# Half of the down weights transposed in the final FFN, with fewer filler transposes and three weight casts on ScalarE

## The chip, the cores and the metric

The kernel runs on one core of a Trainium2 chip. A core has five engines, each with its own queue of instructions that it runs in order: TensorE (PE; its weight loads are listed apart as PEld), VectorE (DVE), ScalarE (ACT), GpSimd (POOL) and SyncE (SP, which only issues transfers here). Engines wait for each other through semaphores. SBUF is the working memory, PSUM the memory that TensorE writes its results to, and DMA moves data between them and the main memory.

The metric is the time of one execution on the device, in microseconds (us); less is better.

## The reference

A graph attention layer and a quantised feed-forward network (FFN), one after the other, each on a layernorm of its input and added to it. 384 nodes, 1024 features, 16 heads of 64, an FFN of width 352.

```python
q = x @ wq.T + bq;  k = x @ wk.T + bk;  v = x @ wv.T + bv
q2 = heads(q @ wiq.T + biq);  k2 = heads(k @ wik.T + bik);  v2 = heads(v @ wiv.T + biv)
mask = full((N, N), -inf); mask[src, dst] = softplus(edge_type_weights)[edge_type - 1]   # diagonal filled
attn = softmax(q2 @ k2^T / 8 + mask)
out = merge(attn @ v2) @ wo.T + bo
...
xq = act_fake_quant(x, clip_x)              # one scale for the whole tensor, from max |x|
gate = xq @ weight_fake_quant(w_gate).T     # one scale per row of a weight, from its max |w|
up   = xq @ weight_fake_quant(w_up).T
h = act_fake_quant(silu(gate) * up, clip_down)
y = h @ weight_fake_quant(w_down).T
...
x = x + gnn(layernorm(x));  x = x + ffn(layernorm(x))
```

`weight_fake_quant` divides a row by its scale, rounds to integers of 8 bits and multiplies by the scale again. The kernel keeps the integers as bf16 for the matmuls and applies the scales to the products.

## The kernel before

**Phase 1 (to about 170 us)** projects q, k, v and the inner q with one level of a Strassen-like scheme. `project2` (L179) handles two blocks of 128 output features at a time with seven products; each product is four accumulating matmuls of 128x192 (L190). In order they use the left operands `wa` left half, `s2`, `wa` right half, `s1`, `wb` left half, `wa` right half (changed in place by the subtraction of L211 after the third product), `wb` right half. DVE makes the sums and differences: those of the weights in `left_sums` (L170, L172, L174), those of the activations in `right_sums` (L158), and the adds of the products (L201, L207, L218, L219, L222). ScalarE makes the first copy (L204) and the one with a bias (L214). Beside that DVE computes for each edge whether a later edge has the same key (L424 to L434), and POOL scatters the edges' values into the mask in main memory (L437) and loads it back (L451).

**The attention phase (to about 325 us)** goes over eight pairs of heads. For a pair it issues on PE, in an order written out by hand, the scores (L625), the transposes of the pair before (L655, copied to SBUF by ScalarE at L657), their products with the values (L663), and as filling work either an inner-k projection (`project2` again, now with two PSUM buffers for the products), an inner-v block (L602) or parts of the output projection (L673). DVE adds the mask and takes the minimum of the negated scores (L631), ScalarE takes the exponential (L635), DVE rescales (L645).

**The FFN's weights** are prepared in between by the generator `ffn_weights` (L523), in fourteen units, here called u0 to u13: three row blocks of the gate weights, three of the up weights, eight of the down weights. A unit's row comes by a DMA on SP's queue (L533) into one of three row buffers, two units ahead. `quantise_rows` (L510) then takes the row maximum on DVE (`wmx`, L512), makes the scale (L513) and its reciprocal (`wrs`, L515) there, quantises to int8 on ScalarE (`w8b`, L518, one buffer) and casts to bf16 on DVE (`wqi`, L520, two buffers). One step later PE transposes the result (L550 for gate and up, eight transposes a unit; L557 for down, three a unit), and ScalarE copies the transposes to `wgT`, `wuT` (L551) or `wdT` (L558, L559). Which step runs when is set by `prepare` (L722) inside the pairs.

The order on PE, SP and POOL is that of the program throughout. The order on DVE and ScalarE is the program's in the first phase's opening and from L758 on; for the FFN's preparation and the attention phase a scheduler places their instructions by its own estimates, each engine still in one fixed order.

**The end (from about 325 us)**: the output projection's last products (L838) with residual and row statistics on DVE (L767 to L820), then the final FFN. There PE transposes the normalised rows (L872), spreads the greatest row maximum over the partitions with one transpose (`all_max`, L129, and a maximum on DVE, L131), and DVE and ScalarE quantise the activations (L902 to L908). Gate and up matmuls (L920) run in four groups; `silu` on ScalarE (L926), the product and its maximum on DVE (L927, L930). The same `all_max` gives the scale of h, h is quantised (L955 to L960), the down matmuls run (L969), DVE scales the products (L973), and `x` is added: the first three blocks on POOL (L977), the last three on DVE (L981), each stored by a DMA on SP's queue (L978, L982). Between these steps `keep_busy` (L874) issues transposes of an identity whose results nobody reads: 14 at L882, 14 at L890, 17 at L939. The PSUM pool `ps_x` hands out four buffers in turn to the transposes of the second row block, the fillers, the up products and every other down product.

Of the kernel before, what the change touches and what calls it, by code (L numbers as in the profile page):

```python
# [24 lines left out]
BF16 = mybir.dt.bfloat16  # L25
# [3 lines left out]
ALU = mybir.AluOpType  # L29
# [3 lines left out]
P = 128  # L33
N = 384
NT = N // P
F = 1024
KC = F // P
# [5 lines left out]
HN = N // 2  # L43
HK = KC // 2
WARM = 36
H = 16
D = F // H
I = 352
ICS = [(0, 128), (128, 128), (256, 96)]
# [12 lines left out]
def gnn_ffn_kernel(ctx: ExitStack, tc: tile.TileContext, a: dict, out: bass.AP):  # L62
    nc = tc.nc
# [6 lines left out]
    rows_p = ctx.enter_context(tc.tile_pool(name="rows", bufs=3))  # L70
# [12 lines left out]
    x = act.tile([P, NT, F], F32, name="actT")  # L83
# [10 lines left out]
    ident = const.tile([P, P], F32)  # L94
# [39 lines left out]
    w_scale = ffn.tile([P, 2, 3], F32)  # L134
    wd_scale = ffn.tile([P, KC], F32)
# [6 lines left out]
    ident_b = const.tile([P, P], BF16)  # L142
# [104 lines left out]
    with ph1_stack:  # L247
# [46 lines left out]
        def turn(t, xn, g):  # L294
            pt = ps_tp.tile([P, 4, P], F32, name="tp")
            for j in range(4):
                c = 4 * g + j
                nc.tensor.transpose(pt[:, j, :], xn[:, c * P : (c + 1) * P], ident)

            for j in range(0, 4, 2):  # L300
                c = 4 * g + j
                nc.scalar.copy(xnT[:, c : c + 2, t * P : (t + 1) * P], pt[:, j : j + 2, :])
# [10 lines left out]
        pt = ps_tp.tile([P, P], F32, name="tp")  # L313
        for _ in range(WARM):
            nc.tensor.transpose(pt, ident, ident)  # L315
# [37 lines left out]
        pt = ps_tp.tile([P, 512], F32, name="tp")  # L353
# [10 lines left out]
        pt = ps_tp.tile([P, 3, EC], F32, name="tp")  # L364
# [138 lines left out]
    ffn_w = ctx.enter_context(tc.tile_pool(name="ffn_w", bufs=1))  # L503
    wgT = ffn_w.tile([P, KC, I], BF16)
    wuT = ffn_w.tile([P, KC, I], BF16)
    wdT = ffn_w.tile([P, 3, F], BF16)
    v2 = act.tile([P, NT, F], F32, name="actT")
    outT = act.tile([P, KC, N], F32, name="actT")

    def quantise_rows(wn, rows, n, scale):  # L510
        mx = small.tile([P, 1], F32, name="wmx")
        nc.vector.tensor_reduce(mx[:rows], wn[:rows, :n], axis=AX.X, op=ALU.max, apply_absolute_value=True)  # L512
        nc.vector.tensor_scalar(scale, mx[:rows], 1.0 / QMAX, None, op0=ALU.mult)  # L513
        rs = small.tile([P, 1], F32, name="wrs")
        nc.vector.reciprocal(rs[:rows], scale)  # L515

        w8b = rows_p.tile([P, F], I8, name="w8b", bufs=1)
        nc.scalar.activation(w8b[:rows, :n], wn[:rows, :n], AF.Copy, scale=rs[:rows])  # L518
        wq = rows_p.tile([P, F], BF16, name="wqi", bufs=2)
        nc.vector.tensor_copy(wq[:rows, :n], w8b[:rows, :n])  # L520
        return wq

    def ffn_weights():  # L523

        units = [(name, m, ic) for m, name in enumerate(("L0_ffn_w_gate", "L0_ffn_w_up")) for ic in range(3)]
        units += [("L0_ffn_w_down", 2, c) for c in range(KC)]
        ahead = []

        def load_row():
            name, m, j = units[len(ahead)]  # L530
            i0, rows = ICS[j] if m < 2 else (j * P, P)
            wn = rows_p.tile([P, F], F32, name="row")
            nc.sync.dma_start(wn[:rows, : F if m < 2 else I], a[name][i0 : i0 + rows, :])  # L533
            ahead.append(wn)

        load_row()
        load_row()
        yield
        for u, (name, m, j) in enumerate(units):
            wn = ahead[u]  # L540
            if len(ahead) < len(units):
                load_row()
            if m < 2:
                i0, rows = ICS[j]
                wT = (wgT, wuT)[m]
                wq = quantise_rows(wn, rows, F, w_scale[:rows, m, j : j + 1])
                yield
                pt = ps_tp.tile([P, KC, P], BF16, name="tp")
                for k in range(KC):
                    nc.tensor.transpose(pt[:, k, :rows], wq[:rows, k * P : (k + 1) * P], ident_b[:rows, :rows])  # L550
                nc.scalar.copy(wT[:, :, i0 : i0 + rows], pt[:, :, :rows])  # L551
            else:
                wq = quantise_rows(wn, P, I, wd_scale[:, j : j + 1])
                yield
                pt = ps_tp.tile([P, 3, P], BF16, name="tp")
                for ic, (i0, rows) in enumerate(ICS):
                    nc.tensor.transpose(pt[:rows, ic, :], wq[:, i0 : i0 + rows], ident_b)  # L557
                nc.scalar.copy(wdT[:, 0:2, j * P : (j + 1) * P], pt[:, 0:2, :])  # L558
                nc.scalar.copy(wdT[:96, 2, j * P : (j + 1) * P], pt[:96, 2, :])  # L559

    prep = ffn_weights()

    next(prep)
    nc.sync.dma_start(biv_b, row_bcast(a["L0_gnn_biv"], F))

    with ExitStack() as ph:
# [19 lines left out]
        def inner_v(c):  # L586

            cs = slice(c * 256, (c + 1) * 256)
            wt = []
            for j in range(2):  # L590
                wt.append(w.tile([P, F], F32, name="wt"))
                nc.sync.dma_start(
                    wt[j].rearrange("p (k o) -> p k o", k=HK),
                    a["wiv"][j * HK : (j + 1) * HK, :, cs].rearrange("k p o -> p k o"),
                )

            def steps():
                for t in range(NT):
                    pm = ps_mm.tile([P, 256], F32, name="mm")
                    for k in range(KC):  # L600
                        k0 = k % HK * 256
                        nc.tensor.matmul(  # L602
                            pm, vT[:, k, t * P : (t + 1) * P], wt[k // HK][:, k0 : k0 + 256],
                            start=(k == 0), stop=(k == KC - 1),
                        )
                        if k < KC - 1:
                            yield
                    nc.vector.tensor_add(v2[:, t, cs], pm, biv_b[:, cs])
                    yield

            return steps()
# [58 lines left out]
        def out_group(wo, t, g, ks, pm):  # L670
            gs = slice(g * 512, (g + 1) * 512)
            for k in ks:
                nc.tensor.matmul(  # L673
                    pm, outT[:, k, t * P : (t + 1) * P], wo[k][:, gs], start=(k == 0), stop=(k == KC - 1)
                )
                yield
# [5 lines left out]

        NP = H // 2

# [3 lines left out]
        for p in range(NP):  # L688
# [4 lines left out]
            if p == NP - 1:  # L693
                early = [(t, g, ps_mm.tile([P, 512], F32, name="mm")) for t, g in ((0, 0), (0, 1))]
                fill, n = (s for t, g, pm in early for s in out_group(wo, t, g, range(NP - 2), pm)), 2 * (NP - 2)
            elif p % 2:
                k2_next, fill = inner_k(p + 1)
                n = 7 * HK + 1
            else:
                fill, n = inner_v(p // 2), NT * KC  # L700
            if p == NP - 2:

                x = act.tile([P, NT, F], F32, name="actT")
# [4 lines left out]
                for t in range(NT):  # L708
                    for g in range(2):
                        gs = slice(g * 512, (g + 1) * 512)  # L710
# [112 lines left out]
        for t in range(NT):  # L823
# [7 lines left out]
            for g, (c0, width) in enumerate(groups):  # L831
                pm = open_groups.get((t, g)) if t < NT - 1 else None
                ks = [NP - 1]
                if pm is None:
                    pool, name = (ps_mm, "mm") if g < 2 else (ps_sc, "sc")
# [14 lines left out]
    with ExitStack() as ph:  # L850
        ff = ph.enter_context(tc.tile_pool(name="ff", bufs=3))
        ps_x = ph.enter_context(tc.tile_pool(name="ps_x", bufs=4, space=PSUM))
# [9 lines left out]
        pt = ps_x.tile([P, 512], F32, name="x")  # L862
# [11 lines left out]
        def keep_busy(n, pool, name):  # L874

            pt = pool.tile([P, P], F32, name=name)
            for _ in range(n):
                nc.tensor.transpose(pt, ident, ident)

        turn(0)  # L880
        turn(1)
        keep_busy(14, ps_x, "x")  # L882
        nc.vector.tensor_scalar(
            xn[:, NT - 1, :512], x[:, NT - 1, :512], mean, rstd, op0=ALU.subtract, op1=ALU.mult
        )
# [1 line left out]
        rx = small.tile([P, 1], F32, name="ar0")  # L887
        nc.vector.reciprocal(rx, sx)
        turn(2)
        keep_busy(14, ps_x, "x")  # L890
        gu_scale = small.tile([P, 2, 3], F32, name="gu_scale")
        nc.gpsimd.tensor_scalar(gu_scale, w_scale, sx, None, op0=ALU.mult)

# [3 lines left out]
        def part(tile, t, g):  # L897
            return tile[:, 4 * g : 4 * g + 4, t * P : (t + 1) * P]

        for g in range(2):  # L900
# [6 lines left out]
            for t in ((2, 0, 1), (0, 1, 2))[g]:  # L907
                nc.vector.tensor_copy(part(xqT, t, g), part(x8, t, g))  # L908


        idle = small.tile([P, 1], F32, name="idle")
        nc.scalar.activation(idle, clip[:, 0:1], AF.Silu)
        for col, ic, c0, width in ((0, 0, 0, N), (1, 1, 0, N), (2, 2, 0, N // 2), (3, 2, N // 2, N // 2)):
            i0, rows = ICS[ic]
# [18 lines left out]
        for g in range(2):  # L933
            pt = ps_tp.tile([P, 4, P], F32, name="tp")
# [1 line left out]
                c = 4 * g + j  # L936
                nc.tensor.transpose(pt[:, j, :], wd_scale[:, c : c + 1].to_broadcast([P, P]), ident)
            nc.scalar.copy(wd_scale_b[:, g * 512 : (g + 1) * 512], pt.rearrange("p a b -> p (a b)"))
        keep_busy(17, ps_x, "x")  # L939
        mx = small.tile([P, 1], F32, name="hmax")  # L940
        scaled = small.tile([P, 4], F32, name="hscaled")
        nc.vector.tensor_tensor_reduce(
# [2 lines left out]
        pt = ps_tp.tile([P, P], F32, name="tp")  # L945
# [15 lines left out]
        last = []  # L961
        for t in range(NT):
            ts = slice(t * P, (t + 1) * P)
            for g in range(2):
                gs = slice(g * 512, (g + 1) * 512)
                pool, name = (ps_mm, "mm") if g == 0 else (ps_x, "x")
# [5 lines left out]
                y = ff.tile([P, 512], F32, name="y", bufs=6)  # L972
# [4 lines left out]
                    nc.gpsimd.tensor_add(y, x[:, t, gs], y)  # L977
                    nc.sync.dma_start(out[t * P : (t + 1) * P, gs], y)  # L978

        for t, gs, y in last:  # L980
            nc.vector.tensor_add(y, x[:, t, gs], y)  # L981
            nc.sync.dma_start(out[t * P : (t + 1) * P, gs], y)  # L982


# [45 lines left out]
```

## Time and profile before

| what | value |
|---|---|
| median of 3 runs | 374.53 us (374.22 to 374.98) |
| the profiled execution, its own time | 375.57 us |
| its span, first to last instruction | 372.7 us |
| mean granted TensorE clock in it | 0.995 |
| busy: PE, DVE, ACT, POOL | 359.5, 257.1, 115.5, 76.0 us |
| the end of the residual stage and the final FFN, first transpose of L872 to end of span | 342.0 to 372.7 us |
| row loads of w_down on the chain that ended last | 3% of the span |

Sums are made against the profiled execution, whose time is 2.87 us above its span. A row of the timeline gives the start in us, the duration in us, the engine, the line, the operation, the tiles (output, then inputs), shapes and count; in square brackets stand the idle time of the engine before it and the instruction that ended it. Records of matmuls in f32 come in pairs, two for an instruction. The matmuls' ends are modelled, so the distance from start to start is the better measure of what one holds of PE.

### The profile page before, as it was taken

Reading aid. Unit: us, or ns where it says so; the run is one execution under the profiler, and the core shown is the slowest. Engines: PE = TensorE matmul, PEld = TensorE weight load, DVE = VectorE, ACT = ScalarE, POOL = GpSimd, SP = SyncE. Lnnn points to the kernel's source line nnn. Section 1 sums busy time; section 2 is a strip of 40 time slices with the busy share of each in tenths; the row PEclk is TensorE's granted clock in tenths of the full one; section 3 lists DMA queues with packets and bytes.
Section 4 is the critical chain, followed back from the end, with each engine's and each line's share of the span. In section 5 each row is a group of like instructions: output and inputs, shape, how many; then the busy total and the mean of one; then the engine's idle time right before and its main releaser. Section 6 shows DMA issues by size and latency. Waiting matters only on the chain.

```text
span 372.7 us, 5875 instructions
## 1 busy us (share of the span) xinstructions
PE 359.5 (96%) x2112; PEld 299.9 (80%) x2113; DVE 257.1 (69%) x785; ACT 115.5 (31%) x275; POOL 76.0 (20%) x81
## 2 busy tenths in 40 slices
PE   8999999999999999989999999999999999999981
PEld 8999999999999998888887868686866545449660
DVE  5788878888889969986497357717492621099665
ACT  2352110000000003023482556445444533033630
POOL 6010355455444543430000000000000000000003
PEclk9999999999999999999999999999999999999998
DMA  7969333443333377551170040050294000000004
GB/s 234 393 249 371 130 115 113 116 134 115 113 113 115 113 267 224 176 152 68 38 233 15 19 133 20 21 170 0 96 381 130 36 0 2 0 0 4 0 0 169
DMA packets 17804, 44.50 MB, mean 119 GB/s; under 512 B 3262, under 2 KB 8400, under 8 KB 17392
## 3 DMA queue, kind: packets, MB, share of 16 engines
q1 hardware_dynamic: 15104, 39.46, 31.4%
q0 software_dynamic: 2672, 4.68, 3.9%
q8 instruction: 16, 0.26, 0.3%
q14 instruction: 12, 0.10, 0.1%
HBM read 41.91 MB, written 2.21 MB: 118 GB/s over the span
## 4 chain that ended last, share of the span: by engine, by line
PE 76%; DVE 16%; DMA 3%; ACT 2%; issue 1%; DVEq 0%; POOL 0%; POOLq 0%; ACTq 0%
PE p L190 33%; PE mm L190 8%; PE mm L602 8%; PE tp L655 4%; PE sc L625 3%; PE sc L663 3%; PE mm L673 3%; PE sc L673 3%; PE mm L307 3%; DMA row<-in_L_ffn_w_down_dram 3%; PE tp L315 2%; DVE wmx L512 1%; DVE e L645 1%; DVE st L774 1%; PE mm L920 1%
## 5 line engine op out<-in xcount | busy, mean ns | idle before, releaser
L437 POOL DMA_INDIRECT mask_d<-value,place x51 | 60.5, 1186 | 65.2 <-DVE place L434 45.9
L190 PE MATMUL p<-actT,wt 128*128 128x192 f32 x360 | 66.2, 327 | 1.0 <-DVE wt L211 1.0
L190 PEld LDWEIGHTS p<-actT,wt 128*128 128x128 f32 x360 | 59.5, 190 | 1.8 <-DVE wt L211 1.5
L602 PE MATMUL mm<-wt,actT 128*128 128x256 f32 x192 | 46.1, 384 | 0.0
L602 PEld LDWEIGHTS mm<-wt,actT 128*128 128x128 f32 x192 | 34.8, 190 | 7.8 <-issue 2.2
L635 ACT ACTIVATE e<-s,mn 128x384 f32<-128x384 f32 x48 | 29.0, 605 | 28.2 <-DVE mn L631 28.1
L631 DVE CUSTOM_DVE_ANT_0 s<-sc,mask 128x384 f32<-128x384 f32 x48 | 24.4, 552 | 15.0 <-PE sc L625 14.9
L190 PE MATMUL p<-x_right,s 128*128 128x192 f32 x176 | 32.2, 326 | 0.0
L190 PE MATMUL p<-x_right,wt 128*128 128x192 f32 x176 | 32.2, 326 | 0.0
L855 POOL MEMSET hT<- 128x384 f32 x1 | 0.4, 418 | 154.7 <-PE sc L663 154.7
L190 PEld LDWEIGHTS p<-x_right,s 128*128 128x128 f32 x176 | 29.2, 190 | 0.0
L190 PEld LDWEIGHTS p<-x_right,wt 128*128 128x128 f32 x176 | 29.2, 190 | 0.0
L657 ACT COPY eTs<-tp 128x384 f32<-128x384 f32 x48 | 20.5, 478 | 25.3 <-PE tp L655 25.3
L424 DVE SCALAR_TENSOR_TENSOR junk<-key_b,key,later 128x384 f32<-128x384 f32 (+3 forms) x51 | 27.5, 539 | 0.0
L204 ACT COPY actT<-p 128x192 f32<-128x192 f32 x15 | 4.8, 321 | 64.7 <-PE p L190 64.7
L201 DVE SCALAR_TENSOR_TENSOR actT<-p,bias,actT 128x192 f32<-128x192 f32 x45 | 18.6, 414 | 7.7 <-PE p L190 4.5
L214 ACT ACTIVATE actT<-p,bias 128x192 f32<-128x192 f32 x15 | 6.3, 420 | 50.8 <-PE p L190 29.3
L655 PEld LDWEIGHTS tp<-ident,e 128*128 128x128 f32 x144 | 17.1, 141 | 4.9 <-issue 2.4
L655 PE MATMUL tp<-ident,e 128*128 128x128 f32 x144 | 19.7, 273 | 0.3 <-ACT eTs L657 0.3
L625 PE MATMUL sc<-k,actT 64*128 64x384 f32 x96 | 20.0, 519 | 0.0
L190 PE MATMUL mm<-actT,wt 128*128 128x192 f32 x96 | 19.0, 330 | 0.0
L645 DVE TENSOR_SCALAR e<-e,rs 128x384 f32<-128x384 f32 x48 | 17.2, 415 | 0.4
(220 smaller groups left out, 593.2 us busy)
## 6 DMA issues: line engine op xcount, KB each, us to landing
wt<-in_wq_dram SPq DMA_DIRECT2D x8, 512.0 KB
wt<-in_wk_dram SPq DMA_DIRECT2D x8, 512.0 KB
wt<-in_wv_dram SPq DMA_DIRECT2D x8, 512.0 KB
wt<-in_wiq_dram SPq DMA_DIRECT2D x8, 512.0 KB
wt<-in_wik_dram SPq DMA_DIRECT2D x8, 512.0 KB
wt<-in_wiv_dram SPq DMA_DIRECT2D x8, 512.0 KB
wt<-in_wo_dram SPq DMA_DIRECT2D x8, 512.0 KB
actT<-in_x_dram SPq DMA_DIRECT2D x6, 512.0 KB
```

The costliest lines, as they stand in the source:

```text
L190: nc.tensor.matmul(z, left[:, k * P : (k + 1) * P], r[:, k, :], start=(k == 0), stop=(k == HK - 1))
L201: nc.vector.scalar_tensor_tensor(dst, z, b, with_, op0=ALU.add, op1=ALU.add)
L424: nc.vector.scalar_tensor_tensor(junk[:, :left], keys[:, (c - k0) * P : (c - k0) * P + left], key[:, c : c + 1], later[:, :left], op0=ALU. ...
L437: ins = nc.gpsimd.indirect_dma_start(out=mask_d, out_offset=bass.IndirectOffsetOnAxis(ap=place[:, c : c + 1], axis=0), in_=value[:, c : c ...
L602: nc.tensor.matmul(pm, vT[:, k, t * P : (t + 1) * P], wt[k // HK][:, k0 : k0 + 256], start=(k == 0), stop=(k == KC - 1),)
L625: nc.tensor.matmul(ps[t, h], q2[hs, t * P : (t + 1) * P], k2[hs, :], start=True, stop=True)
L631: nc.vector.tensor_tensor_reduce(s, ps[t, h], mask[:, t, :], -SCALE, 3.0e38, op0=ALU.add, op1=ALU.min, accum_out=mn[h][:, t : t + 1],)
L635: nc.scalar.activation(e[h][:, t, :], s, AF.Exp, bias=mn[h][:, t : t + 1], scale=-1.0, accum_out=sm[h][:, t : t + 1],)
L645: nc.vector.tensor_scalar(e[h][:, t, :], e[h][:, t, :], rs[:, t : t + 1], None, op0=ALU.mult)
L655: nc.tensor.transpose(pt[:, t * P : (t + 1) * P], e[h][:, t, m * P : (m + 1) * P], ident)
L657: nc.scalar.copy(eT[h][m], pt)
L673: nc.tensor.matmul(pm, outT[:, k, t * P : (t + 1) * P], wo[k][:, gs], start=(k == 0), stop=(k == KC - 1))
```

## The change

Three edits to the FFN's weights and activations, and one to the last add.

- The last four down units (u10 to u13) are cast into a tile of their own, `wd_late`, and not transposed in the attention phase. Their twelve transposes stand in the final FFN: six after the second block of rows has been turned, six after the third. DVE copies them to `wdT` behind the casts of the activations, in four copies.
- The fillers there become 10 and 9, written into a PSUM tile that exists already, where there were 14 and 14; before the transpose that spreads the maximum of h there are 7 where there were 17.
- The casts to bf16 of the three gate units (u0 to u2) are issued on ScalarE in place of DVE.
- The first of the last three adds is issued as `scalar_tensor_tensor` with a factor of 1.0.

```diff
+LATE = 4
...
+    wd_late = ffn_w.tile([P, LATE, I], BF16)
...
-    def quantise_rows(wn, rows, n, scale):
+    def quantise_rows(wn, rows, n, scale, on_scalar=False, wq=None):
...
-        wq = rows_p.tile([P, F], BF16, name="wqi", bufs=2)
-        nc.vector.tensor_copy(wq[:rows, :n], w8b[:rows, :n])
+        if wq is None:
+            wq = rows_p.tile([P, F], BF16, name="wqi", bufs=2)
+        if on_scalar:
+            nc.scalar.copy(wq[:rows, :n], w8b[:rows, :n])
+        else:
+            nc.vector.tensor_copy(wq[:rows, :n], w8b[:rows, :n])
...
-                wq = quantise_rows(wn, rows, F, w_scale[:rows, m, j : j + 1])
+                wq = quantise_rows(wn, rows, F, w_scale[:rows, m, j : j + 1], on_scalar=u < 3)
...
+            elif j >= KC - LATE:
+                quantise_rows(wn, P, I, wd_scale[:, j : j + 1], wq=wd_late[:, j - KC + LATE, :])
+                yield
...
+        def turn_late(j):
+            pl = ps_x.tile([P, 2, 3, P], BF16, name="x")
+            for u in range(2):
+                for ic, (i0, rows) in enumerate(ICS):
+                    nc.tensor.transpose(pl[:rows, u, ic, :], wd_late[:, j + u, i0 : i0 + rows], ident_b)
+            return pl
+
+        def copy_late(j, pl):
+            c0 = (KC - LATE + j) * P
+            for i0, i1, rows in ((0, 2, P), (2, 3, 96)):
+                nc.vector.tensor_copy(
+                    wdT[:rows, i0:i1, c0 : c0 + 2 * P].rearrange("p i (u q) -> p i u q", u=2),
+                    pl[:rows, :, i0:i1, :].rearrange("p u i q -> p i u q"),
+                )
+
+        def keep_turning(n, to):
+            for _ in range(n):
+                nc.tensor.transpose(to, ident, ident)
+
         turn(0)
         turn(1)
-        keep_busy(14, ps_x, "x")
+        late_a = turn_late(0)
+        keep_turning(10, pt[:, :P])
...
         turn(2)
-        keep_busy(14, ps_x, "x")
+        keep_turning(9, pt[:, :P])
+        late_b = turn_late(2)
...
+        copy_late(0, late_a)
+        copy_late(2, late_b)
...
-        keep_busy(17, ps_x, "x")
+        keep_busy(7, ps_x, "x")
...
-        for t, gs, y in last:
-            nc.vector.tensor_add(y, x[:, t, gs], y)
+        for n, (t, gs, y) in enumerate(last):
+            if n == 0:
+                nc.vector.scalar_tensor_tensor(y, x[:, t, gs], 1.0, y, op0=ALU.mult, op1=ALU.add)
+            else:
+                nc.vector.tensor_add(y, x[:, t, gs], y)
```

The compiled order of the instructions moves with it where the scheduler decides. On DVE the maximum of u2 stands where u1's cast was and that of u3 where u2's was; the reciprocals of u2 and u3, and the maxima of u4 and u5, come correspondingly earlier, and u3's cast stands ahead of u6's maximum. On ScalarE u2's quantising stands ahead of a copy with a bias that it followed, u2's cast between two copies of `wgT`, and the quantising of u10, u11 and u12 directly behind each other. SP's and POOL's orders are the same as before.

## The prediction

> **What bounds the kernel now.** I read the page first (its head and the chain that ended last), then the timeline of each stage that the change touches, TensorE (PE) ahead of the others.
>
> ```profile
> span 372.7 us, 5875 instructions
> ...
> PE 76%; DVE 16%; DMA 3%; ACT 2%; issue 1%; DVEq 0%; POOL 0%; POOLq 0%; ACTq 0%
> ```
>
> PE carries the chain except where VectorE (DVE) does; so a step is worth something where it lies on PE with no wait behind it, or on DVE where PE waits. PE's timeline at the end of phase 1 (start, us, engine, line; the idle time before a group and what ended it in brackets):
>
> ```profile
> 146.48 1.46 PE L190 MATMUL p<-right,wt 128*128 128x192 f32 x8
> 148.36 1.57 PE L190 MATMUL p<-actT,wt 128*128 128x192 f32 x8 [0.42 <-DVE wt L211]
> ...
> 152.96 1.57 PE L190 MATMUL p<-right,s 128*128 128x192 f32 x8 [0.43 <-DVE s L172]
> ...
> 158.96 1.57 PE L190 MATMUL p<-actT,wt 128*128 128x192 f32 x8 [0.53 <-DVE wt L211]
> ...
> 167.56 1.57 PE L190 MATMUL mm<-k_right,wt 128*128 128x192 f32 x8 [0.53 <-DVE k L201]
> ```
>
> A product (4 matmuls, 8 records) takes 1.30 us start to start where nothing waits. Here four begin 0.58, 0.59, 0.69 and 0.70 late, and the steps after them are longer by 0.66 together (0.11 three times, 0.23 and 0.10 after the last): 3.2 us, all for DVE, whose queue shows why:
>
> ```profile
> 146.70 0.69 DVE L520 CAST wqi<-w8b 128x1024 bf16<-128x1024 int8 x1
> ...
> 147.63 0.68 DVE L211 TENSOR_TENSOR wt<-wt,s 128x512 f32<-128x512 f32 x1
> ...
> 148.64 0.68 DVE L520 CAST wqi<-w8b 128x1024 bf16<-128x1024 int8 x1
> ...
> 153.37 1.20 DVE L512 TENSOR_REDUCE wmx<-row 128x1 f32<-128x1024 f32 x1
> ...
> 165.96 1.22 DVE L512 TENSOR_REDUCE wmx<-row 96x1 f32<-96x1024 f32 x1 [0.82 <-DMA row<-in_L_ffn_w_up_dram]
> ```
>
> DVE has no pause from 140.3 to 164.2, and the FFN's casts and maxima stand ahead of what PE waits for. The final FFN, all engines:
>
> ```profile
> 357.31 1.89 PEld L878 LDWEIGHTS x<-ident 128*128 128x128 f32 x17
> ...
> 358.03 0.08 DVE L942 DVE_READ_ACCUMULATOR2_ANT hmax<- 128x1 f32 x1
> 359.16 0.14 PEld L129 LDWEIGHTS tp<-ident,hmax 128*128 128x128 f32 x1
> ```
>
> The maximum of h is ready at 358.11, but the transpose that spreads it (L129) queues behind 17 filler transposes until 359.16.
>
> **The change, part by part.** FFN units are u0 to u13 (three gate, three up, eight down).
>
> *Three casts to ScalarE (ACT).* The compiled order of each engine's instructions lets the queue be replayed with the start-to-start times of the rows. Off DVE: u0's and u1's casts, 0.60 each (148.64 to 149.24). But the maxima of u2 and u3 (1.13 each) move up into their places. First stall: L201 takes 146.70, L211 147.03 to 147.71, PE's product starts at its natural 147.78: 0.58 gained. Second: until L172 DVE lost 1.20 and got u3's 1.13, so s2 is ready at the same 152.9 and PE starts at 152.95: what was gained is lost again. Third: now those 1.13 are missing behind, L211 ends at 157.83, natural start 158.26 instead of 158.96; 0.81 with the shorter next step. Fourth: L201 at 167.10 stood behind u5's maximum, which waited for its row; that load was issued at 161.90, after ACT's quantising of u2, whose reciprocal came at 160.50. In the new order the reciprocal comes at about 153.3 and the load at 154.7, so the maximum no longer waits; L201 ends at 165.4, before the natural 166.06: another 0.70 + 0.23 + 0.10. PE then reaches inner V at 169.96 instead of 171.79: 1.83. At 192.69 PE waited another 0.22 behind a DVE queue that begins with u7's row; that queue comes 2.05 earlier (u3's cast stands ahead of u6's maximum now), so 2.0 in all. ACT pays three casts: not in the trace; nearest rows 1.01 (L551, a copy of 128x1024) and 1.15 (L518, 128x1024 to int8), below both 0.72 (L819, half as wide). I take 1.15. They lie in ACT's pauses: 3.69 us before 152.57 for the first two, 2.33 before 182.40 for u2's, which pushes u3's quantising (178.92) back against PE's gain, and u6's row with it: that load comes some 0.9 earlier, not 1.83, and the maximum that waits for it on DVE has the scores of PE behind it with over 1 us to spare (inner V's third add, 185.04 now). If that cover is gone, up to 1.15 is lost there. Bounds of the whole: 0 (everything lost again, as at the second stall) to 3.4 (all stalls gone, with that at 192.69).
>
> *Twelve transposes leave attention.* Units u10 to u13 lose three each. From PE's timeline:
>
> ```profile
> 277.56 1.89 PE L602 MATMUL mm<-wt,actT 128*128 128x256 f32 x8
> 279.76 0.92 PE L655 MATMUL tp<-ident,e 128*128 128x128 f32 x6 [0.30 <-ACT eTs L657]
> ...
> 284.63 0.33 PE L557 MATMUL tp<-ident_b,wqi 128*128 128x128 bf16 x3
> 284.80 1.51 PE L602 MATMUL mm<-wt,actT 128*128 128x256 f32 x6
> ```
>
> A group holds PE 0.17 us (284.63, 301.69), or 0.22 ahead of scores (290.99; 0.26 with the gap of 0.10 before it, less the 0.14 that scores need anyway, 184.80 to 184.94). The one at 272.46 is worth nothing: PE waits at 279.76 for ACT, whose exps hang on a DVE run from 269.08. Sum 0.56; bounds 0 and 0.78. Eight evacuations (0.37 + 0.26 a unit) leave ACT, where they set no end. The new order puts the quantising of u11 and u12 ahead of ACT's exps at 253.40, each behind a DVE cast (one int8 buffer): about 0.24 later, and the rescaled scores end at 256.75 instead of 256.5; their reader is PE at 259.99. Cost 0. SP's and POOL's orders are unchanged.
>
> *They return in the final FFN.* Six bf16 transposes (6 x 0.055 = 0.33) and ten fillers (10 x 0.109) end by 345.3, before the row maximum that PE awaits at 345.55; nine and six more end by 348.3, before DVE's cast at 348.63. Four PSUM copies on DVE: 512 wide between 0.42 (L908, from SBUF) and 0.74 (L973, from PSUM), 256 wide up to 0.42 (L608): at most 2.3 us, starting at 349.96, where DVE idles 2.06 until 352.01. An overhang of 0.3 goes into the 1.34 us that DVE idles before 354.56. Two PSUM buffers of the up product now wait for these copies: needed at 353.90 and 355.22, with the rest of the gate and up matmuls queued behind, and free by 351.2 and 352.3. Cost 0; without the cover up to 2.3.
>
> *Ten fillers fewer before L129.* Seven at 0.109 end at 358.1; the maximum decides at 358.11, plus the 0.06 that L129 took behind the row maximum: 358.17 instead of 359.16. Everything after it follows: 0.99, bounds 0.9 and 1.05.
>
> *One add as a three-operand instruction (L981).* Its first add took 1.15, the others 0.68: it ended 0.55 after GpSimd's last add at 366.53. Whatever this form does, the four last output transfers run back to back:
>
> ```profile
> 367.20:367.40 0.20, 0.00 (x0) 0.00 (x0) 0.20 (x1) 0.00 (x0) 0.00 (x0) 1.00 0.08 31
> 367.40:367.60 0.20, 0.00 (x0) 0.00 (x0) 0.20 (x1) 0.00 (x0) 0.00 (x0) 1.00 0.94 358
> ```
>
> (last columns: DMA share, GB/s; it stays near 1 until 370.1). The first of the four is GpSimd's, so its start is fixed. I take 0; bounds -0.06 (1x form 0.74 against 0.68) and +0.41.
>
> **Sum.** 2.0 + 0.56 + 0.99 + 0 = 3.55 us. The profiled span goes from 372.7 to 369.1, that execution from 375.57 to 372.0; it was 1.04 above the median of the runs, 374.53, which I carry to 371.0.
>
> **The rivals.** *Casts hand the wait on* (0.23): the second stall shows the scheduler filling freed DVE time, and PE already waits at 192.69 and 227.55 behind such queues; against it, the third and fourth stalls lose their cause outright. Casts 0 to 0.8, say 0.4: 374.53 - 1.95 = 372.6. *All of it* (0.08): every DVE stall gone, 3.4 + 0.78 + 1.05 + 0.41 = 5.64: 368.9. It needs L172 1.3 us earlier, which the replay denies. *The clock falls* (0.04): with 19 filler slots fewer TensorE's granted clock could halve before the 64 gate and up matmuls (348.63 to 356.46, 7.83 us); then they take up to 7.83 more and the time is 374.53 - 3.55 + 7.83 = 378.8, slower. It decides only if a pause is long enough: the trace keeps clock 1.00 to 369.0, 3.8 us after the last matmul (365.2), then shows 0.50; the pauses here are 0.4 and 0.4, and 1.6 after L129 as before. The Trainium skill (TensorE: Matmul & The Clock Gate, "What's actually happening") puts the fall after an idle window of some 3.4 us; by that rule, as by the row, nothing falls, and the trace agrees. *A late row* (0.03): u3's maximum at 150.29 now stands ahead of L172; its load, issued at 146.20, shows as DMA traffic until 149.4. If it landed at 155, L172 would come 4.7 us later than replayed: 374.53 - 3.55 + 4.7 = 375.7; the point from which this decides is a landing at 154.
>
> **How the numbers follow.** Forecast 0.62, 371.0, own range 370.2 to 371.9. Shares of the rivals as above. The range 369.7 to 373.1 takes in most of the hand-on case and leaves the other three outside. A measurement here tells about 0.2% (0.75 us) from no change: faster 0.91, same 0.03, slower 0.06.
>
> **What would show it.** Right: PE's waits on L211 and on the k of L201 gone, that on L172 still there; inner V starting near 170.0; L129 about 0.06 after hmax; DMA share near 1 for the last 2.8 us as before. Wrong: a new wait on a wmx behind a row between 150 and 165; a filler group ending after 345.55; the first hT of the final FFN more than 1.3 us late against PE's up product; a granted clock under 1.00 before the last matmul.

## The result, and the profile after

| kernel | median | runs | ratio to before |
|---|---|---|---|
| before, run beside it | 374.22 us (373.26 to 374.98) | 5 | |
| changed | 371.29 us (370.76 to 371.37) | 5 | 0.9921 [0.9905, 0.9937] |

The change takes 2.93 us off; by the interval, between 2.4 and 3.6. The profiled execution of the changed kernel has a span of 369.0 us against 372.7, as forecast to 0.1. That agreement is better than the reasons deserve, as the experiments show: one of the three terms is exact, one depends on the execution, and one is half its size or less in most traces.

The page of the changed kernel, its head and the chain that ended last:

```profile
span 369.0 us, 5835 instructions
...
PE 86%; DVE 11%; issue 1%; ACT 1%; DVEq 0%; POOL 0%; POOLq 0%; ACTq 0%
```

PE has a larger part of the chain (76% before) and DMA none (3%). The lines of the changed kernel lie 1 to 38 higher than those of the kernel before: L191 is L190, L173 is L172, L212 is L211, L515 is L512, L613 is L602, L130 and L132 are L129 and L131, L1017 and L1019 are L981.

TensorE's timeline of the changed kernel, the products that began late before, and the start of inner V:

```profile
147.59 1.56 PE L191 MATMUL p<-actT,wt 128*128 128x192 f32 x8
...
152.76 1.57 PE L191 MATMUL p<-right,s 128*128 128x192 f32 x8 [1.01 <-DVE s L173]
...
158.06 1.46 PE L191 MATMUL p<-actT,wt 128*128 128x192 f32 x8
...
169.85 1.46 PE L613 MATMUL mm<-wt,actT 128*128 128x256 f32 x6
```

Three of the four waits are gone and the one on L173 is longer (0.43 before): the order of events that the replay gave. Inner V starts at 169.85, forecast 169.96. A part of that is luck: 0.19 was gained ahead of the change's first effect (the fourth product of the last but one pair starts at 144.99, 145.18 before), so the casts gained 1.75 by then, where 1.83 was forecast. VectorE's timeline of the same stretch:

```profile
147.85 1.21 DVE L515 TENSOR_REDUCE wmx<-row 96x1 f32<-96x1024 f32 x1
...
150.10 1.20 DVE L515 TENSOR_REDUCE wmx<-row 128x1 f32<-128x1024 f32 x1
...
152.03 0.68 DVE L173 TENSOR_TENSOR s<-s,wt 128x512 f32<-128x512 f32 x1
...
162.87 1.21 DVE L515 TENSOR_REDUCE wmx<-row 96x1 f32<-96x1024 f32 x1
```

These are the maxima of u2, u3 and u5, with the sum that PE waits for behind the first two. u5's no longer waits for its row, whose load went out at 154.50 (161.90 before). On ScalarE the three casts take 1.04, 1.03 and 1.04 us, where 1.15 was assumed; TensorE's timeline shows no wait for ScalarE between inner V and 255. The first of them:

```profile
146.01 1.04 ACT L525 CAST wqi<-w8b 128x1024 bf16<-128x1024 int8 x1
```

The timeline of the final FFN:

```profile
341.09 0.50 PE L895 MATMUL x<-ident_b,wd_late 128*128 128x128 bf16 x6
...
347.14 1.14 DVE L901 COPY wdT<-x 128x512 bf16<-128x512 bf16 x4
...
355.30 0.08 DVE L976 DVE_READ_ACCUMULATOR2_ANT hmax<- 128x1 f32 x1
...
355.86 0.29 DVE L132 TENSOR_REDUCE allmax<-tp 128x1 f32<-128x128 f32 x1 [0.48 <-PE tp L130]
```

The late transposes lie in PE's pauses, the four copies take 1.14 us in all (I had allowed 2.3) in a stretch where DVE idled, and the reduction behind the spread maximum waits 0.48 for PE. In the kernel before it waited 1.47:

```profile
359.58 0.29 DVE L131 TENSOR_REDUCE allmax<-tp 128x1 f32<-128x128 f32 x1 [1.47 <-PE tp L129]
```

### The profile page after: what moved, and what is told of

It reads as the page before. It is cut to its first block, busy times and chain, and to the rows that moved or that the text cites. A ratio compares the mean times of both kernels' runs of the same rounds, so it can differ in the third digit from the quotient of the medians.

```text
span 369.0 us, 5835 instructions
## 1 busy us (share of the span) xinstructions
PE 356.1 (96%) x2093; PEld 297.9 (81%) x2094; DVE 256.1 (69%) x786; ACT 116.1 (31%) x270; POOL 72.6 (20%) x81
## 4 chain that ended last, share of the span: by engine, by line
PE 86%; DVE 11%; issue 1%; ACT 1%; DVEq 0%; POOL 0%; POOLq 0%; ACTq 0%
PE p L191 36%; PE mm L191 10%; PE mm L613 10%; PE sc L636 5%; PE tp L666 4%; PE sc L674 4%; PE sc L684 3%; PE mm L684 3%; PE mm L308 3%; PE tp L316 2%; DVE st L785 1%; PE mm L954 1%; DVE y L1007 1%; PE x L954 1%; DVE actT L780 1%; DVE actT L722 1%
## 5 line engine op out<-in xcount | busy, mean ns | idle before, releaser
L438 POOL DMA_INDIRECT mask_d<-value,place x51 | 57.1, 1120 | 67.5 <-DVE place L435 46.3
L191 PE MATMUL p<-actT,wt 128*128 128x192 f32 x360 | 66.1, 327 | 0.0
L191 PEld LDWEIGHTS p<-actT,wt 128*128 128x128 f32 x360 | 59.6, 190 | 0.3
L613 PE MATMUL mm<-wt,actT 128*128 128x256 f32 x192 | 45.8, 384 | 0.0
L613 PEld LDWEIGHTS mm<-wt,actT 128*128 128x128 f32 x192 | 34.9, 190 | 7.8 <-issue 2.8
L191 PE MATMUL p<-x_right,s 128*128 128x192 f32 x176 | 32.2, 326 | 0.0
L191 PE MATMUL p<-x_right,wt 128*128 128x192 f32 x176 | 32.2, 326 | 0.0
L191 PEld LDWEIGHTS p<-x_right,s 128*128 128x128 f32 x176 | 29.2, 190 | 0.0
L191 PEld LDWEIGHTS p<-x_right,wt 128*128 128x128 f32 x176 | 29.2, 190 | 0.0
L202 DVE SCALAR_TENSOR_TENSOR actT<-p,bias,actT 128x192 f32<-128x192 f32 x45 | 18.7, 416 | 7.5 <-PE p L191 5.1
L191 PE MATMUL mm<-actT,wt 128*128 128x192 f32 x96 | 19.0, 330 | 0.0
L619 DVE TENSOR_TENSOR actT<-mm,biv_b 128x256 f32<-128x256 f32 x12 | 5.0, 421 | 18.5 <-PE mm L613 18.5
```

The lines of the kernel that those rows point to most:

```text
L191: nc.tensor.matmul(z, left[:, k * P : (k + 1) * P], r[:, k, :], start=(k == 0), stop=(k == HK - 1))
L202: nc.vector.scalar_tensor_tensor(dst, z, b, with_, op0=ALU.add, op1=ALU.add)
L438: ins = nc.gpsimd.indirect_dma_start(out=mask_d, out_offset=bass.IndirectOffsetOnAxis(ap=place[:, c : c + 1], axis=0), in_=value[:, c : c ...
L613: nc.tensor.matmul(pm, vT[:, k, t * P : (t + 1) * P], wt[k // HK][:, k0 : k0 + 256], start=(k == 0), stop=(k == KC - 1),)
```

## The experiments

Twelve kernels, each timed beside the kernel before on the same chip. Two executions of one kernel differ by most of a microsecond (spans of 369.0 and 369.9 for the changed kernel), also at places that the change doesn't touch, so the second table compares stretches that begin and end at the same instruction in every trace.

| kernel | median us | ratio to before, 95% |
|---|---|---|
| casts alone | 372.81 | 0.9969 [0.9950, 0.9988] |
| casts back | 372.77 | 0.9960 [0.9946, 0.9973] |
| u3's maximum later | 372.68 | 0.9955 [0.9938, 0.9972] |
| three maxima later | 369.99 | 0.9885 [0.9869, 0.9900] |
| six maxima later | 369.96 | 0.9867 [0.9846, 0.9888] |
| seventeen fillers | 372.82 | 0.9956 [0.9937, 0.9975] |
| none late | 371.75 | 0.9919 [0.9901, 0.9938] |
| no fillers | 371.95 | 0.9912 [0.9888, 0.9935] |
| changed, again | 371.65 | 0.9909 [0.9889, 0.9929] |
| plain add | 371.43 | 0.9909 [0.9890, 0.9928] |
| two adds on GpSimd | 370.96 | 0.9898 [0.9880, 0.9917] |
| six later and two adds | 368.76 | 0.9836 [0.9816, 0.9856] |

Stretches of the traces in us, each the difference of two starts: A from the fourth product of the last but one pair of phase 1 (145.18 before) to inner V (171.79); B in attention, from the transposes of L655 at 259.99 before to those at 314.94, as the difference to before (54.95); C from the first gate matmul to the reduction of L131 (L132 changed); D from that reduction to the end of the span. The profile gives the span to 0.1 us, so D is good to 0.05.

| kernel | A | B | C | D |
|---|---|---|---|---|
| before | 26.61 | 0 | 10.94 | 13.12 |
| changed | 24.86 | -0.21 | 9.95 | 13.14 |
| changed, again | 24.86 | -0.13 | 9.96 | 13.09 |
| plain add | 24.83 | -0.18 | 9.96 | 13.09 |
| casts alone | 25.55 | +0.10 | 10.94 | 13.15 |
| casts back | 26.64 | -0.56 | 9.95 | 13.10 |
| u3's maximum later | 25.87 | -0.26 | 9.95 | 13.14 |
| three maxima later | 23.80 | -0.44 | 9.95 | 13.11 |
| six maxima later | 23.49 | -0.41 | 10.23 | 13.14 |
| seventeen fillers | 25.88 | -0.33 | 10.94 | 13.17 |
| none late | 24.86 | -0.02 | 9.95 | 13.18 |
| no fillers | 24.86 | -0.16 | 9.94 | 13.23 |
| two adds on GpSimd | 24.86 | -0.26 | 9.95 | 12.30 |
| six later and two adds | 23.48 | -0.49 | 10.24 | 12.29 |

**Casts alone.** The kernel before with the one parameter:

```diff
-                wq = quantise_rows(wn, rows, F, w_scale[:rows, m, j : j + 1])
+                wq = quantise_rows(wn, rows, F, w_scale[:rows, m, j : j + 1], on_scalar=u < 3)
```

> The kernel before with the casts of u0, u1 and u2 on ScalarE and nothing else. My theory (two of the four DVE stalls go, one is handed on, PE gains some 1.9 us by inner V and another 0.2 at the scores after it): 2.0 us under the kernel before, 1.7 to 2.3; in the trace PE waits at L172's sum and not on L211 or on k of L201. Rival 'casts hand the wait on': 0.4 us, 0 to 0.8, with a wait on L211 or L201 left.

By the ratio it is 1.2 us faster (0.4 to 1.9): between the forecast and "hand on", with an interval that reaches into both. What tells them apart is the trace, where the waits on L211 and L201 are gone. Its span is 1.7 shorter. Its timeline shows where the rest went, on VectorE and on TensorE (L512 and L190 as before):

```profile
148.68 1.22 DVE L512 TENSOR_REDUCE wmx<-row 96x1 f32<-96x1024 f32 x1 [0.93 <-DMA row<-in_L_ffn_w_gate_dram]
...
153.60 1.57 PE L190 MATMUL p<-right,s 128*128 128x192 f32 x8 [1.75 <-DVE s L172]
```

u2's maximum stood in DVE's queue for 0.93 us, waiting for its row, with the sum behind it: the stall grew from 1.0 to 1.75. That row was asked for at 141.85 and landed at 148.68. In the kernel before the maximum came at 150.30; moved up to 147.8 it has no room left.

**Casts back.** The changed kernel with `on_scalar=False`.

> The changed kernel with all casts on VectorE again. If the parts add up: 2.0 us slower than the changed kernel, so 0.9 to 1.2 us under the kernel before (its 2.9 less 2.0), and the four PE waits of the kernel before are back (0.42, 0.43, 0.53, 0.53 us). Rival 'the late transposes and the fillers bring more than their 1.55': 1.6 to 2.0 us under the kernel before.

1.5 us under before (1.0 to 2.0), between the two; A is 26.64, that of the kernel before, and the four waits are there again (0.38, 0.42, 0.53, 0.60). So A belongs to the casts and to nothing else in the change.

**u3's maximum later, three later.** Whether it is the amount of DVE's work or its order is told apart by moving maxima and nothing else, with an ordering edge (one instruction must stand behind another) for the scheduler:

```diff
+        if after is not None:
+            tc.add_manual_dep(
+                ins.ins, after.ins.name,
+                mybir.DependencyInfo(mybir.DependencyClass.NoSync, mybir.DependencyReason.DATA), reason="behind s2",
+            )
```

`after` is for the one kernel the sum of L173 at 152.03, for u3; for the other the next such sum, for u3, and adds of L202 of the first inner K, for u4 and u5.

> The changed kernel with u3's row maximum held behind the sum of L173 that PE waits for at 152.76; the scheduler then moves u4's maximum forward into the place between that sum and L212. My theory (it is the order of DVE's queue that sets these waits, and its replay can be trusted): the wait on L173 (1.01) goes, but L212 ends 1.13 later, at 158.7, and PE's product behind it starts at 158.8 instead of 158.06; nothing later has room to win that back before inner V: 0.7 us slower than the changed kernel, 0.5 to 0.9. Rival 'the amount of DVE work ahead of inner V sets it, whatever its order': no difference, within 0.3. Rival 'the maximum ahead of L173 alone costs': 1.0 us faster.

> The changed kernel with three row maxima held back: u3's behind the last sum of L173 in phase 1 (into the place that u4's has now), u4's and u5's behind the second sum of L202 of the first inner K, where DVE idles from 168 to 183. The amount of DVE work is the same. My theory: no PE wait before inner V is left, inner V starts 1.0 us earlier (168.8), and the time is 0.7 to 1.1 us under the changed kernel. Rival 'the amount of DVE work sets it': no difference. Rival 'the wait comes back at the scores' (u4's and u5's maxima end at 170.9, ahead of the scores' first reader): 0 to 0.3 faster.

TensorE's timeline with u3's maximum later (L193 and L214 are L191 and L212 there):

```profile
159.43 1.57 PE L193 MATMUL p<-actT,wt 128*128 128x192 f32 x8 [1.61 <-DVE wt L214]
```

The wait on L173 is gone, and a longer one stands at the next subtraction (L212, L214 there), behind u4's maximum that the scheduler put in the free place. A is 1.01 longer than in the changed kernel (forecast 0.7), and the ratio 0.34% higher. With three maxima later A is 23.80, 1.06 shorter (forecast 1.0); no wait is left between 142 and inner V, and the ratio is 0.36% lower. The same work in three orders gives 25.87, 24.86 and 23.80: it is the order. The rival "the amount" is out, and so is the answer that the second stall can't be had.

**Six later.** u0's maximum behind L219 of the last pair but one, u2's behind L173, besides the three.

> The kernel with three row maxima held back, and the three before them held back too: u0's behind the sum of L219 of the last pair but one (u1's follows it), u2's behind the sum of L173 that PE waits for at 152.76. My theory (a maximum waits on DVE for its row's transfer, in some executions by 0.8 us longer than in others, and everything behind it in DVE's queue waits with it, PE at last): no PE wait for DVE between 130 and 170 in any execution, so 0.3 to 0.9 us under the kernel with three maxima held back, and a narrower spread of times. Rival 'the rows come in time in most executions': no difference from it, within 0.2.

The PE waits for DVE between 130 and 170 are gone in both traces with this order (this kernel and the last one), and the times lie within 0.7 us (369.33 to 370.02) where those with three later span 1.7. The medians are the same (369.96 and 369.99), and the ratios' intervals overlap: the further gain isn't shown by the times. C is 0.28 longer in both traces with this order: there ScalarE's first quantising of the activations starts 0.53 us after the reciprocal of their scale and is released by the third block's transposes, where it starts 0.26 after it with three later. Why the order of the maxima brings that is open.

**Seventeen fillers.** `keep_busy(17, ...)` in the changed kernel.

> The changed kernel with 17 fillers again ahead of the transpose that spreads h's maximum. My theory (that transpose queues behind the fillers in PE's order): 0.99 us slower than the changed kernel, so 1.9 under the kernel before; the reduction behind it (L132) waits 1.47 for PE again instead of 0.48. Rival 'the fillers were hidden by another wait': no difference.

C is 0.99 longer, exactly, with the wait of 1.47 at L132 back. The time is 1.3 us above the changed kernel's by the ratios (0.9956 and 0.9921); a difference of 0.99 lies within their intervals. The profiled execution also has a stall of 1.76 at L173, u2's maximum having waited 1.34 for its row.

**None late.** All eight down units turned in attention again:

```diff
-            elif j >= KC - LATE:
-                quantise_rows(wn, P, I, wd_scale[:, j : j + 1], wq=wd_late[:, j - KC + LATE, :])
-                yield
...
-        late_a = turn_late(0)
-        keep_turning(10, pt[:, :P])
+        keep_busy(14, ps_x, "x")
```

> The changed kernel with all eight down units turned in attention, as before, and 14 and 14 fillers in the final FFN in place of the late transposes and their copies; casts, the last 7 fillers and the last add as changed. My theory (the twelve transposes cost PE 0.57 in attention, and in the final FFN they are free): 0.57 us slower than the changed kernel, 0.4 to 0.7, so 2.4 under the kernel before, with all of the difference between the stalls at 172 and 340. Rival 'the late copies cost DVE or PSUM something in the final FFN': less than 0.3 slower.

The ratio, 0.9919, is that of the changed kernel; a difference of 0.57 would be 0.15%, inside the intervals, so the times can't tell. The traces can: in B the three traces with all twelve transposes in attention have -0.02, 0 and +0.10, the eleven without have -0.13 to -0.56, on average -0.31. So the transposes bring some 0.3, not 0.56. The groups at 284.63, 290.99 and 301.69 brought their share: the stretch from 279.76 on is 0.60 to 0.62 shorter in each of the eleven. It is given back ahead of that. The changed kernel, VectorE's add of the residual and TensorE's wait behind it:

```profile
267.89 0.69 DVE L722 TENSOR_TENSOR actT<-actT,wt 128x512 f32<-128x512 f32 x1 [0.29 <-issue]
...
277.64 0.92 PE L666 MATMUL tp<-ident,e 128*128 128x128 f32 x6 [0.75 <-ACT eTs L668]
```

and the same two in the kernel with none late (L718, L662):

```profile
268.29 0.69 DVE L718 TENSOR_TENSOR actT<-actT,wt 128x512 f32<-128x512 f32 x1
...
277.99 0.92 PE L662 MATMUL tp<-ident,e 128*128 128x128 f32 x6 [0.29 <-ACT eTs L664]
```

The add is the first reader of x's transfer, issued at 264.19. With none late DVE reached it at 268.29, 3.34 after the issue, and didn't wait; in the changed kernel DVE idled until 3.70 after. The exps and the transposes hang on DVE's run behind it, so PE waits 0.46 longer at 277.64. The profile calls the idle time "issue"; that it is the transfer is what the order of the queue suggests and was not tried by itself. The eleven traces bear it out. In seven of them VectorE idles 0.16 to 0.36 ahead of this add, and B is -0.13 to -0.33; in the four where it doesn't idle (casts back, three later, six later, six later and two adds) B is -0.41 to -0.56. So where the add finds its data, the term comes near its forecast. Why the transfer takes longer in most of these traces stays open.

**No fillers.** All three calls taken out.

> The changed kernel without any filler in the final FFN (10, 9 and 7 taken out), so that PE has pauses of about 1.4, 1.4 and 1.2 us there. My theory (pauses so short don't lower the granted clock, and fillers end before what PE waits for): the clock stays 1.00 from 340 to the last matmul, and the time is that of the changed kernel, within 0.3 us. Rival 'the clock falls in a pause': granted clock under 1 between 341 and 356 and 1 to 8 us slower.

The stretches C and the one before it are those of the changed kernel (9.94; 5.70 from the second block's transposes to the first gate matmul, against 5.69), and the time is the same. But the granted clock did fall, later. Windows of that kernel (busy time of PE, PEld, DVE, ACT and POOL with counts, granted clock, DMA share, GB/s):

```profile
359.00:360.00 1.00, 0.78 (x4) 0.50 (x6) 0.73 (x3) 0.12 (x1) 0.00 (x0) 1.00 0.00 0
...
361.00:362.00 1.00, 1.00 (x4) 0.32 (x3) 0.48 (x2) 0.00 (x0) 1.00 (x2) 0.50 0.00 0
...
364.00:365.00 1.00, 0.75 (x4) 0.14 (x2) 0.86 (x2) 0.00 (x0) 0.41 (x1) 1.00 0.69 262
```

and its TensorE timeline:

```profile
357.14 0.29 PE L130 MATMUL tp<-ident,hmax 128*128 128x128 f32 x1 [0.68 <-ACT wd_scale_b L970]
359.23 0.60 PE L1000 MATMUL mm<-wdT,hq 128*128 128x512 bf16 x2 [1.79 <-DVE hq L991]
...
361.55 1.48 PE L1000 MATMUL x<-wdT,hq 128*128 128x512 bf16 x3
```

Without the seven, two pauses (0.68 and 1.79) stand with one transpose between them, and a down group takes 1.48 where it takes 0.81 in the changed kernel, from about 360.3 to 363.8. The forecast that nothing falls is wrong here, in this one profiled execution; that the time is the same is luck, as what sets the end shows. It cost D only 0.1, which led to the last question.

**What sets the end.** In that trace PE's last group of down matmuls starts 1.7 us later behind L132 than in the changed kernel, and SP is through with the transfers 1.1 later; if they set the end, as the prediction said, D would be longer by as much, not by 0.1. The last adds of the changed kernel, and the instructions of the end of its program (number, shortest/median/longest in ns, first and last start); the DRAIN rows stand at the end of the engines' queues:

```profile
359.09 3.72 POOL L1011 TENSOR_TENSOR y<-actT,y 128x512 f32<-128x512 f32 x3 [15.19 <-DVE y L1007]
...
362.21 1.15 DVE L1017 SCALAR_TENSOR_TENSOR y<-actT,y 128x512 f32<-128x512 f32 x1
...
L1064 POOLq DRAIN  x3: 46/97/7847, 360.4 to 368.7; - x3
L1064 SPq DRAIN  x3: 7/7/7, 367.2 to 368.5; - x3
```

SP's first drain, behind the transfers, is at 367.2; GpSimd's drain, begun at 360.4, lasts until 368.25, 5.4 us after its last add (362.81). The same 5.4 stand in the kernel before (366.53 to 371.96), and without fillers GpSimd's adds were not late: they began 3.2 us behind L132 in either kernel. So I took one add from GpSimd, and for the other question the three-operand form away:

```diff
-                if t * 2 + g >= 3:
+                if t * 2 + g >= 2:
```

> The changed kernel with the first of the last three adds in its two-operand form again. My theory (both forms wait for GpSimd's add the same way): that add takes 1.15 us as before, no difference to the changed kernel, within 0.2 us. Rival 'the three-operand form brings something': up to 0.4 us slower.

> The changed kernel with two of the six last adds on GpSimd and four on VectorE, in place of three and three. My theory since the first eight runs (the end is set by GpSimd, which is done with its queue 5.4 us after its last add, and not by the last transfers, which end 1.1 us ahead of that): GpSimd's last add ends 1.2 us earlier, all of VectorE's adds take 0.68 or less, and the span is 0.6 to 0.9 us shorter behind h's maximum (13.1 from the reduction of L132 to the end becomes 12.2 to 12.5). Rival, as the prediction had it ('the back-to-back transfers set the end'): 0.2 to 0.3 us longer.

The plain add changes nothing: ratio 0.9909 as that of the changed kernel beside it, 1.15 us for the first add in either form. With two adds on GpSimd D is 12.30, 0.84 shorter, as forecast, and not 0.2 longer as by the transfers. Its end:

```profile
359.82 2.50 POOL L1011 TENSOR_TENSOR y<-actT,y 128x512 f32<-128x512 f32 x2 [15.18 <-DVE y L1007]
...
L1064 POOLq DRAIN  x3: 46/97/7290, 360.4 to 368.6; - x3
L1064 SPq DRAIN  x3: 7/7/7, 368.1 to 368.4; - x3
```

GpSimd's drain ends at 367.7, and SP's now comes last, at 368.1: the next bound. Against the changed kernel beside it the step is 0.4 us by the ratios and 0.7 by the medians (370.96 and 371.65); the intervals overlap, so it is the trace that shows it. VectorE's first add has the three-operand form, and GpSimd is done before it starts:

```profile
362.94 0.68 DVE L1017 SCALAR_TENSOR_TENSOR y<-actT,y 128x512 f32<-128x512 f32 x1
```

**Changed, again** tells how steady the second stall is; **six later and two adds** puts the finds together.

> The changed kernel itself, profiled in another execution. My theory (u2's row maximum now stands ahead of the sum of L173 and waits for its row's transfer as long as that takes): the PE wait on L173 is 1.0 or, where the row lands late, up to 1.8 us, and the stretch from the product at 145 to inner V lasts 24.9 to 25.9 us; the time stays 0.6 to 1.0% under the kernel before. Rival 'the order of the queue alone sets that wait': 1.0 us and 24.9 again.

> Six row maxima held back, and two of the last adds on GpSimd. If the two add up: 0.6 to 0.9 us under the kernel with six maxima held back, so about 1.5% under the kernel before. Rival 'the transfers set the end': 0.2 us over it.

The changed kernel showed 1.0 and 24.86 again. Over all eight traces with this order of maxima ahead of L173 (changed twice, casts alone, plain add, seventeen, none late, no fillers, two adds) u2's row was late in three: by 0.34, 0.93 and 1.34. The last kernel is the best: 1.64% under before (1.44 to 1.84), 2.9 us under the changed kernel on the same chip (368.76 and 371.65), with D 12.29 and A 23.48.

## Why the prediction was right, and where it was not

- **Fillers, 0.99: right.** C is 9.95 or 10.94 with seven or seventeen, within 0.01, in every trace but the two with six maxima held back.
- **Casts, 2.0: right in mechanism, the size depends on the execution.** In the profiled one A gives 1.75 and the wait at 192.69 another 0.22, together 1.97. The step that missed is "the maxima of u2 and u3 move up into their places" at a cost of DVE time alone. Moving u2's up by 2.5 us took it to where its row lands, and three of eight executions waited there, of which two paid 0.7 and 1.0 in A; the mean of A over the eight is 25.07, so the casts bring 1.54 + 0.22 = 1.8 on average. "A late row" was on the list of rivals, but for u3's row, which never waited.
- **The second stall, "what was gained is lost again": right**, and the replay forecast both other orders to 0.3. That it can't be helped ("needs L172 1.3 us earlier, which the replay denies") holds for the scheduler's order only; three ordering edges did it.
- **Twelve transposes, 0.56: half of it, whole only where a transfer has landed.** The three later groups gave 0.61. Taking out the group at 272.46, put at nothing, goes with a loss of about 0.3 on average (0.28 to 0.47 where the first add of x waits for its transfer, 0.06 to 0.20 where it doesn't): that add lies on the path that I had named as deciding there. That the two profiles differ by just 0.57 between 192.69 and the final FFN is luck: 0.35 of it arises between 214 and 231, where the other traces lie from 0.47 below the kernel before to 0.28 above it, whatever their order.
- **Late work in the final FFN, 0: right.** The copies end at 348.3 in the changed kernel, ahead of the first product of `silu` at 349.29, and C is the same with and without them.
- **The last add, 0: the value right, the reason wrong.** The form of the add did nothing: it takes 1.15 us either way. "Whatever this form does, the four last output transfers run back to back" is true, but they don't set the end; GpSimd's drain does, as the kernel with two adds shows. GpSimd's last add fixes both, so a faster add of VectorE would have gained nothing either; that is argued, not tried. The add's 1.15 beside GpSimd's adds, and 0.68 without them, agree with the Trainium skill (SBUF — State Buffer, "Who interferes with whom"): a VectorE operation with two inputs from SBUF is blocked while a GpSimd operation that reads SBUF holds the port pair that they share.
- **"The clock falls": right not to expect it here, for a reason that doesn't hold.** "It decides only if a pause is long enough" is not what the traces show. The longest pause is 1.79 us with the seven fillers and without them, and the clock fell before the last matmul only without them. What fits all fourteen traces is how much PE works in a window of 3.41 us; that is read from them afterwards and was not tried by itself, and the last section has the figures.

The terms as measured, 1.8 + 0.3 + 0.99 = 3.1, stand against 2.93 measured and 3.55 forecast.

## What to carry to other kernels

An instruction that a scheduler moves up in an in-order queue takes its wait along: before a cast or a copy is taken out, look at what moves into its place, when the data of that arrive, and who is queued behind. A difference of half a microsecond between two profiles is no proof of a term of that size; compare stretches with fixed ends over several traces, including those of kernels that leave the stretch alone. And look at which engine is done last at the end of a program: here one add off GpSimd took 0.84 us off the stretch D, while the form of VectorE's add changed nothing.

## What the runs showed of the hardware that was not expected

- GpSimd's drain at the end of the program ends 5.4 us after its last add, in the kernel before, the changed one and the one with two adds alike, and the span 0.7 to 0.8 after the later of it and SP's.
- Without fillers the granted clock fell to 0.50 at about 360.3, 1.1 us after PE had resumed work at 359.23, and stayed there for some 3.4 us: the fall follows the pauses with a delay, and work that has begun doesn't stop it. The Trainium skill (TensorE: Matmul & The Clock Gate, "What's actually happening") has PE's activity judged over free-running windows of about 3.4 us. The traces agree in the length: the first stretch at clock 1.00 is 354.99, 358.40 or 361.81 us long in each of the fourteen, and the one at 0.50 in this trace 3.41, all whole multiples of 3.413. They don't agree that a window must be idle, as the same section has it. With windows of 3.413 us counted back from the first fall of each trace, PE was busy for 1.42 us or less in the window just ahead of the fall in all fourteen (1.42 without fillers, from 356.93 to 360.35), and for 1.62 or more in every window before that one (1.62 in the changed kernel, from 355.31 to 358.72). If this is what decides, the point lies between 1.42 and 1.62 us of 3.41 in these traces, and the margin of the changed kernel is thin.
- A row of 384 KB (u2's) asked for at 141.85 was there at 148.68, 6.8 us later, in the kernel with casts alone; with the plain add it took 6.1 us (141.18 to 147.28), with seventeen fillers 7.1 (141.28 to 148.43). What held it up was not looked into.
